# Zero products of 28 columns instead of 506 in the score accumulator of a conv and attention kernel

## The chip, the core and the metric

One core of a Trainium2 chip runs the whole program in one launch. The metric is device time in microseconds (us), from the start to the end of an execution. A run's time is one such execution, and the time before is the median of three.

Four engines work side by side, each through its own queue in order: TensorE (PE; weight loads are shown apart as PEld), VectorE (DVE), ScalarE (ACT) and GpSimd (POOL). SyncE (SP) issues most DMAs.

## The reference

Sixteen images of 128 channels and 28x28 pixels pass through four layers: an L1-distance convolution, two 3x3 convolutions with quantised weights and activations, then on 784 tokens an image an additive attention with a mixture of experts, and a linear attention with a spectral filter. The change concerns the scores of the additive attention:

```python
def _L2_attn_ref(B, W, v):
    Wi = jnp.einsum('bnd,ed->bne', B, W)
    scores = jnp.einsum('d,bijd->bij', v, jnp.tanh(Wi[:, None, :, :] + Wi[:, :, None, :]))
    attn = jax.nn.softmax(scores, axis=-1)
    C = jnp.einsum('bij,bjd->bid', attn, B)
    return C
```

A score is symmetric in i and j, so that half of them are enough.

## The kernel before

**Stages.** The images go in pairs. For each pair the distance convolution makes taps on DVE (lines 1139 and 1141) and ACT (line 1137), and PE sums them (line 1126). Beside the distances of a later pair, the remaining layers of earlier images are woven in: the quantised convolutions, the scores, the attention, the experts, the linear attention and the spectral filter (lines 1019 and 1022). In the trace the scores begin at 1156 us. From about 10390 us on no distances are left, and the code calls that stage "alone".

**Buffers.** Taps and, in the stage alone, blocks of tanh values share a ring of 10 buffers (RING). Rows of tanh values have 14 (ROWS). The score accumulator `sp` is one bank of the on-chip accumulation memory (PSUM, which PE writes and DVE and ACT read): 128 partitions x 512 columns, taken anew from a pool of one buffer for every block.

**Scores of one image.** `wi` holds the 784 projected tokens and, after them, the first 504 again. `scores(b)` walks through NT = 7 blocks of TB = 112 tokens. A block is four groups of Q = 28 tokens, and group j has the 32 partitions from 32j on. For m = 0 to 27 the four tokens Qj + m of a block each get a row: tanh of `wi` over a window of WIN = 394 columns that begins at the token itself. Beside the distances ACT makes the rows one by one (line 727), with the token as bias. In the stage alone DVE adds (line 720) and ACT takes the tanh of four rows at once (line 722). `products_of` multiplies the row by v on PE (line 710). The slice of `vz` that is loaded as weights has v in column m and zeros elsewhere, so that partition m of the group receives the row and the other 31 have zeros added. The product lands on columns Qj + m to Qj + m + 393.

**The first row of a block.** As each row lands one column further right than the one before, the accumulator has to be defined over all columns first. At m = 0, four products with zero weights (line 706) are written with `start=True` over all 506 columns, one to each group; the row products then only add.

**The end of a block.** After m = 27 DVE multiplies the 504 columns `sp[:, :SPAN]` by a mask `near` into `sc` (line 738, and line 740 where the window runs over the end of the image). The next block's zero products overwrite the same bank, so they wait for this.

**Order.** The lanes of the planner (`Lane`, `rows`, `ahead`, `behind`) lay down a traced order of all work: taps of the next step, PE sums of this one, products that are due, then other lanes. `in_traced_order` (line 1179) pins that order on PE alone. On DVE, ACT and SP the build chooses the order, from its own estimate of when instructions are ready.

Of the kernel before, what the change touches and what calls it, by code (L numbers as in the profile page):

```python
# [8 lines left out]
F32 = mybir.dt.float32  # L9
# [8 lines left out]
P = 128  # L18
# [46 lines left out]
TB, NT, Q = 112, 7, 28  # L65
# [3 lines left out]
WIN = T // 2 + 2  # L69
SPAN = T // 2 + TB  # L70
# [69 lines left out]
def cols(ap, lo, n):  # L140

    return ap[:, lo // Q * 32 : (lo + n) // Q * 32].rearrange("p (n c) -> p n c", c=32)[:, :, :Q]


def in_rows(ap):

    return ap.rearrange("p (n c) -> p n c", c=Q)
# [23 lines left out]
def kernel(ctx: ExitStack, tc: tile.TileContext, a: dict, out: bass.AP):  # L171
    nc = tc.nc
# [8 lines left out]
    pss = ctx.enter_context(tc.tile_pool(name="pss", bufs=1, space=PSUM))  # L181
# [21 lines left out]
    def slot(n, name):  # L203
        return ring.tile([P, 4 * WIN], F32, tag="d", name=name)[:, :n]
# [215 lines left out]
    vz = const.tile([P, 64], F32, name="vz")  # L420
# [271 lines left out]

    products = []

    def scores(b):


        while b not in state:
            yield
        wi = state[b][3]  # L700

        def products_of(sp, ib, m, rows):
            if m == 0:

                for j in range(4):
                    nc.tensor.matmul(sp[32 * j : 32 * j + 32, : SPAN + 2], vz[:, :32],  # L706
                                     wi[:, ib * TB : ib * TB + SPAN + 2], start=True, stop=False, skip_group_check=True)
            for j in range(4):
                lo = Q * j + m
                nc.tensor.matmul(sp[32 * j : 32 * j + 32, lo : lo + WIN], vz[:, 32 - m : 64 - m], rows[j],  # L710
                                 start=False, stop=m == Q - 1, skip_group_check=True)

        for ib in range(NT):
            sp = pss.tile([P, 512], F32, tag="sp", name=f"sp{b}_{ib}")
            for m in range(Q):
                i = ib * TB + m
                if stage["alone"]:
                    th = slot(4 * WIN, f"th{b}_{ib}_{m}").rearrange("p (a b) -> p a b", b=WIN)
                    for j in range(4):
                        nc.vector.tensor_scalar(th[:, j, :], wi[:, i + Q * j : i + Q * j + WIN],  # L720
                                                wi[:, i + Q * j : i + Q * j + 1], None, ALU.add)
                    nc.scalar.activation(th, th, AF.Tanh)  # L722
                    rows = [th[:, j, :] for j in range(4)]
                else:
                    rows = [rows_pool.tile([P, WIN], F32, tag="row", name=f"row{b}_{i + Q * j}") for j in range(4)]
                    for j in range(4):
                        nc.scalar.activation(rows[j], wi[:, i + Q * j : i + Q * j + WIN], AF.Tanh,  # L727
                                             bias=wi[:, i + Q * j : i + Q * j + 1])
                products.append(lambda sp=sp, ib=ib, m=m, rows=rows: products_of(sp, ib, m, rows))
                yield  # L730
            while products:
                products.pop(0)()
            while ib == 0 and b and b - 1 not in attended:
                yield
            lo = ib * TB
            n = min(SPAN, T - lo)
            dst = sc[:, ib, :]
            nc.vector.tensor_tensor(cols(dst, lo, n), in_rows(sp[:, :n]), in_rows(near[:, :n]), ALU.mult)
            if n < SPAN:
                nc.vector.tensor_tensor(cols(dst, 0, SPAN - n), in_rows(sp[:, n:SPAN]), in_rows(near[:, n:]), ALU.mult)  # L740
        scored.add(b)
# [308 lines left out]
    for b in range(B):  # L1050
        chain.add(attend(b), experts(b), linear_attention(b), normed(b)) if b + 1 == B else chain.add(
            *([head(1)] if b == 0 else []), attend(b), experts(b), linear_attention(b), normed(b),
            *([head(b + 2)] if b + 2 < B else []))
        conv_out.add(spectral(b))
    units = [scores(b) for b in range(B)]
    due = {"units": 0.0}

# [157 lines left out]
```

## Time and profile before

| what | us |
|---|---|
| median of three runs | 12013.93 |
| lowest and highest run | 12013.17, 12015.77 |
| the profiled execution's own time | 12013.72 |
| its span, first to last instruction | 12012.0 |
| DVE busy | 10731.9 |
| ACT busy | 10263.3 |

The profile is of one execution, and the span leaves out 1.72 us around the instructions. Busy time of PE is a union of pipelined matmuls whose ends are modelled, so it is more than the time in which PE streams columns. Of an instruction group the profile gives its line, engine, operands, shape and count; every float32 product stands there as two matmuls, each with a weight load. Thus 448 zero products (16 images x 7 blocks x 4 groups) are 896 matmuls of line 706, eight to a block, and there are 112 blocks.

### The profile page before, as it was taken

What the parts mean: (1) busy time and instruction counts of PE and PEld (TensorE: products, weight loads), DVE (VectorE), ACT (ScalarE), POOL (GpSimd) and SP (SyncE); (2) the same over time, 40 slices, a digit from 0 to 9 for tenths busy, and PEclk for the clock granted to TensorE, in tenths of its full rate; (3) what the DMA queues carried; (4) which work ended last, traced back from release to release, by engine and by line L of the source; (5) the groups of instructions that cost most, each with busy time, mean ns of one, the idle gap of its engine ahead of it and who ended that gap; (6) DMA issues with size and microseconds to landing.
All of it is one profiled execution on the core that took longest, in us unless ns stands there. A gap on an engine that the chain in (4) does not pass through costs nothing. (4 is left out here: it accounts for less than half of the span.)

```text
span 12012.0 us, 240466 instructions
## 1 busy us (share of the span) xinstructions
PE 11409.5 (95%) x99948; PEld 5214.0 (43%) x99948; DVE 10731.9 (89%) x15051; ACT 10263.3 (85%) x14568; POOL 186.2 (2%) x144
## 2 busy tenths in 40 slices
PE   8989999999999999999999999999999999999999
PEld 3333333444444444444444444444444444454446
DVE  9898789899999999899999999999999889988882
ACT  8884998979979899797998979889898898988882
POOL 0000000000000000000000000000000000000000
PEclk9999999999999999999999999999999999999999
DMA  0110000010110101001010110101110111011113
GB/s 24 58 32 5 1 1 6 17 34 27 33 32 18 35 28 32 24 28 33 26 38 17 31 33 25 31 26 31 34 31 19 29 31 34 27 54 51 54 54 97
DMA packets 376034, 372.49 MB, mean 31 GB/s; under 512 B 40296, under 2 KB 362144, under 8 KB 374944
## 3 DMA queue, kind: packets, MB, share of 16 engines
q1 hardware_dynamic: 374512, 355.35, 10.4%
q8 instruction: 787, 12.89, 0.4%
q14 instruction: 303, 2.48, 0.1%
q10 hardware_dynamic: 432, 1.77, 0.0%
HBM read 340.19 MB, written 16.78 MB: 30 GB/s over the span
## 5 line engine op out<-in xcount | busy, mean ns | idle before, releaser
L727 ACT ACTIVATE row<-wi 128x394 f32<-128x394 f32 x9904 | 5297.0, 625 | 254.1 <-PE sp L710 251.8
L1126 PE MATMUL acc<-d,sel_m 128*32 128x392 f32 x38656 | 5217.3, 502 | 144.2 <-DVE d L1141 133.3
L1139 DVE TENSOR_SCALAR d<-pad,w 128x1568 f32<-128x1568 f32 x4832 | 4783.5, 1031 | 456.9 <-PE acc L1126 454.3
L1126 PE MATMUL acc<-d,sel_a 128*32 128x392 f32 x18176 | 4502.8, 500 | 71.1 <-ACT d L1137 68.8
L1137 ACT ACTIVATE d<-pad,w 128x1568 f32<-128x1568 f32 x2272 | 3581.7, 1609 | 597.7 <-PE acc L1126 581.0
L1141 DVE SCALAR_TENSOR_TENSOR d<-pad,w,d 128x1568 f32<-128x1568 f32 x2112 | 3863.1, 1846 | 8.7
L1126 PEld LDWEIGHTS acc<-d,sel_m 128*32 128x32 f32 x38656 | 1714.0, 111 | 2121.2 <-issue 1653.9
L710 PE MATMUL sp<-row,vz 128*32 128x394 f32 x19808 | 2086.9, 495 | 1.1 <-ACT row L727 1.1
L1126 PEld LDWEIGHTS acc<-d,sel_a 128*32 128x32 f32 x18176 | 1349.4, 110 | 1111.1 <-issue 857.7
L1019 PE MATMUL u<-band,up 128*128 128x392 f32 (+3 forms) x8192 | 1752.9, 355 | 16.4 <-ACT us L1029 14.0
L1019 PEld LDWEIGHTS u<-band,up 128*128 128x128 f32 x8192 | 1330.0, 190 | 964.6 <-issue 281.2
L710 PEld LDWEIGHTS sp<-row,vz 128*32 128x32 f32 x19808 | 728.1, 110 | 1052.9 <-issue 791.1
L722 ACT ACTIVATE th<-th 128x1576 f32<-128x1576 f32 x660 | 969.8, 1521 | 118.4 <-DVE th L720 109.7
L720 DVE TENSOR_SCALAR th<-wi 128x394 f32<-128x394 f32 x2640 | 923.3, 420 | 12.0 <-PE sp L710 9.2
L1022 PE MATMUL out<-us,mat 128*128 128x392 f32 (+1 forms) x2048 | 923.6, 534 | 0.0
L1029 ACT COPY us<-u 128x392 f32<-128x392 f32 x1024 | 491.4, 480 | 480.6 <-PE u L1019 478.5
L710 PE MATMUL sp<-th,vz 128*32 128x394 f32 x5280 | 514.1, 503 | 47.7 <-ACT th L722 47.5
L884 DVE SCALAR_TENSOR_TENSOR t<-ex,gate,t 128x128 f32<-128x128 f32 x896 | 310.7, 347 | 83.9 <-PE ex L880 75.7
L1022 PEld LDWEIGHTS out<-us,mat 128*128 128x128 f32 x2048 | 311.7, 192 | 21.3 <-issue 8.3
L710 PEld LDWEIGHTS sp<-th,vz 128*32 128x32 f32 x5280 | 136.8, 109 | 340.7 <-issue 168.0
L880 PE MATMUL ex<-ew,xt 128*128 128x512 f32 x448 | 236.0, 609 | 37.1 <-DVE t L884 33.2
L795 PE MATMUL av<-vx,sc 128*128 128x129 f32 x1568 | 202.4, 282 | 37.3 <-DVE sc L784 18.7
(257 smaller groups left out, 4415.9 us busy)
## 6 DMA issues: line engine op xcount, KB each, us to landing
band<-band SPq DMA_DIRECT2D x1024, 196.0 KB, 2.4
mat<-mat SPq DMA_DIRECT2D x1024, 64.0 KB, 2.0
L_conv_w<-q_L_conv_w SPq DMA_DIRECT2D x16, 576.0 KB
ew<-in_L_ffn_expert_w_dram SPq DMA_DIRECT2D x16, 512.0 KB
eb<-eb_rows SPq DMA_DIRECT2D x16, 448.0 KB, 4.2
x<-in_x_dram SPq DMA_DIRECT2D x8, 784.0 KB
band<-band_out SPq DMA_DIRECT2D x32, 196.0 KB, 1.9
xr<-in_x_dram SPq DMA_DIRECT2D x8, 784.0 KB, 4.1
```

The lines of the kernel that those rows point to most:

```text
L710: nc.tensor.matmul(sp[32 * j : 32 * j + 32, lo : lo + WIN], vz[:, 32 - m : 64 - m], rows[j], start=False, stop=m == Q - 1, skip_group_chec ...
L720: nc.vector.tensor_scalar(th[:, j, :], wi[:, i + Q * j : i + Q * j + WIN], wi[:, i + Q * j : i + Q * j + 1], None, ALU.add)
L722: nc.scalar.activation(th, th, AF.Tanh)
L727: nc.scalar.activation(rows[j], wi[:, i + Q * j : i + Q * j + WIN], AF.Tanh, bias=wi[:, i + Q * j : i + Q * j + 1])
L884: nc.vector.scalar_tensor_tensor(t[:, i, :], q[:, e * P : (e + 1) * P], gate[:, g : g + 1], t[:, i, :], ALU.mult, ALU.add)
L1019: nc.tensor.matmul(q[:, P * i : TH], up[:, to ^ odd, i, :], t[:, :w], start=i == 0, stop=i == 3)
L1022: nc.tensor.matmul(acc[:, lag:TH], m0, u[:, : TH - lag], start=False, stop=n is None and not copied)
L1029: nc.scalar.copy(u[:, :TH], q[:, :TH])
L1126: nc.tensor.matmul(accs[c][32 * j : 32 * j + 32, :NCK], sel[kind][:, 31 - m : 63 - m], d[:, 14 * c : 14 * c + 14, :], start=False, stop=n ...
L1137: nc.scalar.activation(d, window(pad, k, 0, 2 * HW), AF.Abs, bias=w0[:, k, f : f + 1], scale=-1.0)
L1139: nc.vector.tensor_scalar(d, window(pad, k, 0, 2 * HW), w0[:, k, f : f + 1], None, ALU.max)
L1141: nc.vector.scalar_tensor_tensor(d, window(pad, k, 0, 2 * HW), w0[:, k, f : f + 1], d, ALU.max, ALU.add)
```

## The change

The zero products cover 28 columns a group instead of 506: the columns Qj + 394 to Qj + 421, which the first row does not reach and later rows of the group do. The first row's products are now written with `start=True`. The accumulator is one fixed tile for the whole kernel, cleared once by DVE, and columns that no product of a group reaches keep that zero. The number of products is the same, and so are the rows, the weights and the mask multiplication.

```diff
+    sp = pss.tile([P, 512], F32, name="sp")
+    nc.vector.memset(sp, 0.0)
+
     def scores(b):
...
-        def products_of(sp, ib, m, rows):
-            if m == 0:
-
-                for j in range(4):
-                    nc.tensor.matmul(sp[32 * j : 32 * j + 32, : SPAN + 2], vz[:, :32],
-                                     wi[:, ib * TB : ib * TB + SPAN + 2], start=True, stop=False, skip_group_check=True)
+        def products_of(m, rows):
+            for j in range(4):
+                if m == 0:
+
+
+                    hi = Q * j + WIN
+                    nc.tensor.matmul(sp[32 * j : 32 * j + 32, hi : hi + Q], vz[:, :32], wi[:, :Q],
+                                     start=True, stop=False, skip_group_check=True)
             for j in range(4):
                 lo = Q * j + m
                 nc.tensor.matmul(sp[32 * j : 32 * j + 32, lo : lo + WIN], vz[:, 32 - m : 64 - m], rows[j],
-                                 start=False, stop=m == Q - 1, skip_group_check=True)
+                                 start=m == 0, stop=m == Q - 1, skip_group_check=True)
 
         for ib in range(NT):
-            sp = pss.tile([P, 512], F32, tag="sp", name=f"sp{b}_{ib}")
             for m in range(Q):
...
-                products.append(lambda sp=sp, ib=ib, m=m, rows=rows: products_of(sp, ib, m, rows))
+                products.append(lambda m=m, rows=rows: products_of(m, rows))
```

## The prediction

> **What bounds the kernel now.** I read the page's busy times first, then its chain of waits, then the costliest groups, and then went to the blocks' first rows.
>
> ```profile
> PE 11409.5 (95%) x99948; PEld 5214.0 (43%) x99948; DVE 10731.9 (89%) x15051; ACT 10263.3 (85%) x14568; POOL 186.2 (2%) x144
> PE 30%; DVE 11%; ACT 5%; issue 1%; POOL 0%; DMA 0%; POOLq 0%; ACTq 0%; DVEq 0%
> L727 ACT ACTIVATE row<-wi 128x394 f32<-128x394 f32 x9904 | 5297.0, 625 | 254.1 <-PE sp L710 251.8
> L1126 PE MATMUL acc<-d,sel_m 128*32 128x392 f32 x38656 | 5217.3, 502 | 144.2 <-DVE d L1141 133.3
> L1139 DVE TENSOR_SCALAR d<-pad,w 128x1568 f32<-128x1568 f32 x4832 | 4783.5, 1031 | 456.9 <-PE acc L1126 454.3
> L1137 ACT ACTIVATE d<-pad,w 128x1568 f32<-128x1568 f32 x2272 | 3581.7, 1609 | 597.7 <-PE acc L1126 581.0
> ```
>
> All three engines are close to full, PE most. DVE stood still for 454 us and ACT for 581 until PE freed a tap buffer; PE stood still for 133 until DVE had made a tap. So PE leads, but not alone. The chain's shares add up to 47% because the trace could be followed back only to about 6400 us; of those 47 points PE has 30, DVE 11 and ACT 5. Less PE work is therefore worth more than half its length, and not all of it.
>
> Next, the matmuls by shape, of the whole span:
>
> ```profile
> L710 PE MATMUL sp<-row,vz 128*32 128x394 f32 x19808 | 2086.9, 495 | 1.1 <-ACT row L727 1.1
> L706 PE MATMUL sp<-wi,vz 128*32 128x506 f32 x896 | 124.8, 590 | 6.3 <-DVE sc L740 5.9 <-DVE sc L738 0.3
> ```
>
> The zero products almost never wait (6.3 us in all): DVE has usually emptied the bank in time. Then the chain of waits around one block's start shows what four zero products cost PE:
>
> ```profile
> 9323.25 2.77 PE acc L1126 x32
> 9326.02 0.85 PE sp L706 x8
> 9326.87 1.32 PE sp L710 x16
> 9328.19 1.65 PE u L1019 x8
> ```
>
> Columns: start, length, line, matmuls. The eight matmuls take 0.85 us from start to start, as PE runs the four groups together: their modelled durations (590 ns each) overlap. I asked for the chain at each of the 38 block starts from 6400 to 10390 us, and 21 had this picture; at the others DVE or ACT carried the chain. In the stage alone:
>
> ```profile
> by line: PE sp L710 27.9%; PE u L1019 24.4%; PE out L1022 11.3%; DVE th L720 10.8%; ACT th L722 5.1%; PE ex L880 2.9%; PE av L795 2.5%; issue 1.6%; PE sp L706 1.3%; PE conv_ps L395 1.1%; DVE mx L771 0.7%; PE qk L909 0.7%; PE tc_n L646 0.6%;
> ```
>
> 1.3% of these 1300 us (10390 to 11690) is 16.9 us, which is 20 of the stage's 23 blocks at 0.85 us.
>
> **What the Trainium skill says.** (1) "TensorE: Matmul & The Clock Gate", section "Wait — 56ns, not 53.3ns?": two matmuls never start less than about 25 ns apart, however short. Inside a group of four this trace has starts within 0.02 us of each other for four (1150.80 to 1150.82 us in the timeline)[...], so I use 25 ns for a bound alone. (2) Same page, "The mechanism": weight loads pass running matmuls only where the row group differs. The trace says otherwise for column groups: four loads for the rows stand in 0.13 us of PEld beside running sums. (3) "PSUM — Partial Sum Buffer", "The four PSUM rules": a starting matmul clears the written-marks of its whole bank in its quadrant, but not the data. So the first row's start clears the marks that the zero products just set, and the second row overwrites a zero where it would have added to one. By that page the sums come out the same; no run here shows it yet. (4) Same page, "PSUM bank collisions raise a hardware error": PE must not write a bank and quadrant that DVE reads. So the 28-column products need the same wait on lines 738 and 740 as the 506-column ones.
>
> **The change part by part.**
>
> *Zero products.* Of line 706 and line 710 the mean matmuls are 590 and 495 ns, or 587 and 494 by the medians of the two lines' own views: 93 ns for 112 columns, 0.83 ns a column. 506 columns stream for 420 ns, twice for the two matmuls of a product: 0.84 us, as the chain's 0.85 says. 28 columns stream for 23 ns, 0.05 us in all. No row of the trace has so short a product on 32 columns of weights. From below the cost is 0.05 us, if weight loads and starts hide. From above it is two rounds of weight loads, 2 x 0.13 = 0.26 us; eight starts at the page's 25 ns would be 0.20, an estimate. I take 0.15. The quad gets shorter by 0.70 us (0.59 to 0.80), and 112 of them by 78 us of PE (66 to 90).
>
> *What of this reaches the end.* Beside the distances there are 89 blocks (712 matmuls by the windows' counts), of which 21/38 = 55% lie on the chain: 89 x 0.55 x 0.70 = 34 us. For the first 51 blocks I use the same share, since PE is about as busy there (943 to 972 us of each 1000 between 2000 and 9000 us). In the stage alone 20 x 0.70 = 14 us. Together 48 us, if no parallel path takes over. One does, in part. A saving passes from PE to DVE only as far as DVE had been waiting: the waits of line 1139 are 454.3 us over 375 times, 1.2 us each. Where PE's next wait is for DVE (133.3 us over 117 times, 1.1 each) or for a row of ACT, the saving is simply waited away. Both happen within a few microseconds of a block's start. I let 0.6 of the 48 through, a choice between 0.2 (nearly all lost at the next wait) and 1: 29 us.
>
> *Start flag on the first row, narrower reading of `wi`, one fixed bank.* Nothing: the row products have the same columns, PE's in-order queue separates them from the zeros, and the one buffer of the pool was the same bank already. The wait for DVE moves along with the zero products. Queued behind it on PE are the four rows of m = 0 and then sums; today it costs 6.3 us in the whole span, and could be up to 0.70 us longer where PE now arrives earlier, which is in the 0.6.
>
> *The clearing.* One DVE instruction on 512 columns near the start; its nearest row, the mask multiplication of 504 columns, takes 0.68 us. It is done long before 1156 us. At most 0.7 us, with DVE's taps queued behind it; I put it at nothing.
>
> *Order on DVE and ACT.* PE's order is pinned, the others' are not, and the build works them out from estimates that include PE's length. The trace shows that it departs from the written order:
>
> ```profile
> 1486.61 0.62 DVE L738 TENSOR_TENSOR sc<-sp,near 128x448 f32<-128x448 f32 x1 [7.34 <-PE sp L710]
> 1487.16 1.03 DVE L1139 TENSOR_SCALAR d<-pad,w 128x1568 f32<-128x1568 f32 x1
> 1488.10 0.21 DVE L740 TENSOR_TENSOR sc<-sp,near 128x56 f32<-128x56 f32 x1
> ```
>
> A tap of 1.03 us stands between lines 738 and 740, which follow each other in the code. A shorter quad can move such a tap or a row at any of the 112 blocks, for better or worse; I take zero, with 30 us either way for the range.
>
> Sum: the profiled execution's 12013.72 (span 12012.0 and 1.72 around it), less 29, is 11984.7. The median shown is 0.21 above the profiled execution, so 11985.
>
> **The rivals.**
>
> *A, part of the chain's worth (forecast): 11985.* For it: PE's 30 of 47 points, 21 of 38 block starts. Against: so many short waits both ways. Its own range, 0.2 to 0.9 of the 48 us with the quad's bounds: 11966 to 12004.
>
> *B, all of it or more: 48 to 60 us, 11958.* PE would have to lead nearly everywhere. DVE and ACT waited for PE far longer than PE for them, which speaks for it; DVE at 92 to 94% busy beside the distances speaks against.
>
> *C, waited away: 12007.* DVE is the true limit beside the distances, and the quad only brings PE sooner to its next wait. Then only about half of the stage alone's 14 us is left. For it: 17 of 38 block starts were not on PE's chain. Against: DVE's 454 us of waiting.
>
> *D, slower: 12041.* The build's new order puts a tap of line 1139 (1.03 us) ahead of what PE needs next, at DVE's queue around the block's start, in half of the blocks: 112 / 2 x 1.03 = 58 us lost against 29 gained, net 29 slower. It decides from a mean loss of 29 / 112 = 0.26 us a block on. For it: the order of 1487 us above. Against: nothing that prefers bad places to good ones.
>
> **How the numbers follow.** A 0.45, B 0.17, C 0.16, D 0.22. About 0.2%, 24 us, is what a measurement can tell from no change here. A is beyond that in 0.72 of its cases (0.32) and B in all: faster 0.49. C with the rest of A and the small end of D: same 0.27. The larger part of D and its tail: slower 0.24. The range runs from B's far end with 30 us of order luck, 11930, to D with some 15 more, 12055; one in twenty is left out below, some three in twenty above.
>
> **What would show it.** Right: line 706 as 28-column matmuls whose eight take 0.1 to 0.25 us from start to start; PE's busy time some 70 us lower; line 1139's wait for PE lower, and PE's waits for DVE and ACT higher by 30 to 50 us; equal counts on every line. Wrong: a quad above 0.4 us (the floor mis-sized), line 706 waiting far more than 6.3 us for lines 738 and 740, or PE's busy time down with the span unchanged (C). For D, DVE and ACT queues in another order and new waits of line 1126 or line 710.

## The result, and the profile after

The changed kernel takes 11972.85 us (median of 6 runs, 11971.38 to 11975.57) against 12014.41 us before (6 runs, 12013.17 to 12018.26). The ratio is 0.9965, with a 95% interval of 0.9953 to 0.9978: faster by 42 us, where 29 were forecast. The profiled execution took 11972.2 us with a span of 11970.3. Lines behind the change stand four to five numbers further down: 706 is now 711, 710 is 715, 722 is 726, 1126 is 1130, 1137 is 1141 and 1139 is 1143.

The page after, busy time and the two groups that wait for tap buffers:

```profile
PE 11347.5 (95%) x99948; PEld 5198.5 (43%) x99948; DVE 10727.9 (90%) x15052; ACT 10260.9 (86%) x14568; POOL 186.8 (2%) x144
L1143 DVE TENSOR_SCALAR d<-pad,w 128x1568 f32<-128x1568 f32 x4832 | 4780.7, 1030 | 438.2 <-PE acc L1130 429.0
L1141 ACT ACTIVATE d<-pad,w 128x1568 f32<-128x1568 f32 x2272 | 3578.9, 1608 | 570.0 <-PE acc L1130 555.2
```

PE does as many matmuls as before, and DVE one instruction more, the clearing. DVE and ACT work as long as before. What got shorter is the wait of these two groups for PE, by 25 and 26 us (454.3 and 581.0 before). Matmuls by shape show the edit itself:

```profile
L711 PE MATMUL sp<-wi,vz 128*32 128x28 f32 x896 | 31.3, 194 | 6.1 <-DVE sc L744 5.8 <-DVE sc L742 0.3
```

The matmuls' wait for the mask multiplication is as it was (6.1 us, before 6.3), now on a 28-column matmul. The chain of waits around one block's start (columns: start, length, line, matmuls):

```profile
9294.38 2.77 PE acc L1130 x32
9297.15 0.06 PE sp L711 x8
9297.20 1.33 PE sp L715 x16
```

The neighbours have kept their lengths (2.77, and 1.33 for 1.32), and the eight zero matmuls take 0.06 us from start to start, where they took 0.85. That is 0.79 us a block, 88 us over the 112 blocks if each is like this one. So 42 of 88 us reached the end.

Where? The tanh over four rows marks the beginning of the stage alone, in which no distances are left. Its line in the views of that line, before and after (the numbers after the colon are the shortest, median and longest in ns, then come first and last start in us):

```profile
core 0 of [0], span 12012.0 us
L722 ACT ACTIVATE th<-th x660: 1499/1519/1580, 10385.7 to 11676.0; 128x1576 f32<-128x1576 f32 x165
```

```profile
core 0 of [0], span 11970.3 us
L726 ACT ACTIVATE th<-th x660: 1495/1519/1580, 10346.4 to 11635.4; 128x1576 f32<-128x1576 f32 x165
```

The stage begins 39.3 us earlier, and from there to the end it lasts 1626.3 us before and 1623.9 after. Nearly the whole gain arises beside the distances. The stage in which 20 of 23 blocks' zero products lay on the chain gives 2.4 us. That was not forecast, and the experiments start from it.

One thing besides the edit itself had changed. PE's order is pinned, but on ACT 790 of some 14,600 instructions, and on DVE some 2,100 of 15,052, stand elsewhere in the queue than before: on ACT nearly all by one to five places, on DVE three in four of them. The two causes, shorter products and another order, can be taken apart, since an order can be prescribed.

### The profile page after: what moved, and what is told of

Same layout as the page of the kernel before. It is cut to its first block, busy times and chain, and to the rows that moved or that the text cites. A ratio compares the mean times of both kernels' runs of the same rounds, so it can differ in the third digit from the quotient of the medians.

```text
span 11970.3 us, 240357 instructions
## 1 busy us (share of the span) xinstructions
PE 11347.5 (95%) x99948; PEld 5198.5 (43%) x99948; DVE 10727.9 (90%) x15052; ACT 10260.9 (86%) x14568; POOL 186.8 (2%) x144
## 5 line engine op out<-in xcount | busy, mean ns | idle before, releaser
L715 PE MATMUL sp<-th,vz 128*32 128x394 f32 x5280 | 517.8, 504 | 58.8 <-ACT th L726 58.4
```

## The experiments

The theory was that the shorter zero products bring the gain by themselves, by a fixed part of each microsecond saved; its rivals, that the new order on DVE and ACT takes a good part of the gain away, or brings it.

### One cause at a time

Both orders were written into kernels as lists, for DVE, ACT and SP, in the way the code pins PE:

```diff
     in_traced_order(tc, (mybir.EngineType.PE,))
+    in_given_order(tc)
```

```python
for engine, text in GIVEN.items():
...
    for k, by in enumerate(moved):
        i = mine[k + by]
        if last is not None:
            tc.add_manual_dep(
                i, last,
                mybir.DependencyInfo(mybir.DependencyClass.NoSync, mybir.DependencyReason.DATA), reason="order",
            )
        last = i.name
```

The changed kernel in the order of the kernel before:

> The changed kernel, with DVE, ACT and SP held to the order in which the build of the kernel before put them. Theory (the shorter zero products do it, the new order nothing): as the changed kernel, 11973, between 11966 and 11980, with the stage alone (about 1298 us) again no shorter. Rival 1 (the new order gave part of the gain away, above all in the stage alone): about 11960 or less, the stage alone some 12 us shorter. Rival 2 (the new order brought part of the gain): 11985 or more.

Measured: 11983.06 us against 12015.69, ratio 0.9973 (0.9962 to 0.9984): 32.6 us faster. That is neither what the theory said nor what the first rival did; it lies 2 us from what the second said, that the new order brought part of the gain.

The kernel before in the order of the changed one:

> The kernel before with its 506-column zero products, with DVE, ACT and SP held to the order of the changed kernel's build. Theory (order is worth nothing): 12014, between 12007 and 12021. Rival 1 (the new order costs): 12026 or more. Rival 2 (it gains by itself): 12002 or less.

Measured: 12014.20 us against 12015.69, ratio 0.9999 (0.9990 to 1.0007), as the theory said. On the long products the new order is worth nothing in sum, within an interval of some 10 us either way.

```profile
core 0 of [0], span 12012.3 us
L722 ACT ACTIVATE th<-th x660: 1494/1519/1568, 10381.7 to 11677.1; 128x1576 f32<-128x1576 f32 x165
```

The stage alone begins 4.0 us earlier than before and lasts 1630.6 us, 4.3 longer. These are single executions, so whether the sum hides a small gain and a small loss stays open.

The fixed bank and its clearing alone:

```diff
+    sp = pss.tile([P, 512], F32, name="sp")
+    nc.vector.memset(sp, 0.0)
...
-            sp = pss.tile([P, 512], F32, tag="sp", name=f"sp{b}_{ib}")
```

> The kernel before with one fixed bank, cleared once, and the 506-column zero products as they were. Theory: the bank is worth nothing, 12014, between 12009 and 12019. Rival (the fixed bank spares waits on PE, whose line of zero products has 51 semaphore instructions of 51 ns before the change and 3 after): 2.6 us or more faster, down to about 12005.

Measured: 12016.06 us against 12015.69, ratio 1.0000 (0.9992 to 1.0009). The semaphore instructions of the zero products' line, 51 ns each, do fall from 51 to 3 with the bank alone, but no gain is measured: the theory held.

The changed kernel beside the others again:

> The changed kernel itself, beside the others on one chip. All theories: 11973, between 11969 and 11980. What it is for: if it stands below the run with short products in the old order (11983) by 5 us or more again, the new order is worth that much; if the two are level, it is not.

Measured: 11972.91 us against 12015.22, ratio 0.9966 (0.9953 to 0.9978). It is 10 us below the run with the short products in the old order (11983.06), as the changed kernel in the result was (11972.85). The old order was measured on another chip, and the intervals of the two ratios overlap, but no execution of the one kernel does with those of the other: at most 11977.79 us here and at least 11979.08 there, while the kernel before differs by 0.5 us between the two. So 42 us are some 33 from the edit and some 9 from the new order, which on the long products brought 1.5 us, within the noise. The run in the old order shows where the 9 come from:

```profile
core 0 of [0], span 11977.4 us
L726 ACT ACTIVATE th<-th x660: 1497/1519/1603, 10360.1 to 11641.4; 128x1576 f32<-128x1576 f32 x165
```

In the old order the stage alone begins 25.6 us earlier than before and lasts 1617.3 us, 9.0 less than before. The new order therefore helps by 13.7 us beside the distances and costs 6.6 us in the stage alone (single executions; this one is 4 us below its kernel's median). PE's waits for the tanh in that stage agree. The first two lines are of the kernel before, 10392 to 11690 us; the next two of the changed kernel, 10353 to 11650 us; the last two of the run in the old order, 10366 to 11656 us. Columns: total us, times, longest.

```profile
PEld sp L710 <- ACT th L722: 137.2, 171, 3.0
PE sp L710 <- ACT th L722: 47.5, 76, 2.3
```

```profile
PEld sp L715 <- ACT th L726: 158.7, 196, 3.0
PE sp L715 <- ACT th L726: 58.4, 94, 2.5
```

```profile
PEld sp L715 <- ACT th L726: 144.0, 176, 3.0
PE sp L715 <- ACT th L726: 52.7, 81, 2.5
```

With the short products PE waits longer for ACT in this stage than before, and in the new order longer than in the old.

### Both orders, each where it is good

If the reading by stage holds, the new order up to the stage alone and the old order from there on must be faster than either. The lists of DVE and ACT were joined at the first tanh of four rows.

> The changed kernel with the orders of DVE and ACT of its own build up to the stage alone, and those of the build before from there on. Theory (beside the distances the new order helps by 14 us, in the stage alone it costs 6): 11966, between 11961 and 11971. Rival (the two orders' effects aren't a matter of the stage, single profiles mislead): as the changed kernel, 11973, or above.

Measured: 11965.75 us against 12015.22, ratio 0.9959 (0.9946 to 0.9971).

```profile
core 0 of [0], span 11964.0 us
L726 ACT ACTIVATE th<-th x660: 1498/1519/1599, 10346.8 to 11629.7; 128x1576 f32<-128x1576 f32 x165
```

It begins the stage alone where the changed kernel does and lasts there, at 1617.2 us, what the run in the old order does. A second session:

> The mixed order once more, with the 28-column zero products. Theory (its 11966 was the order's doing): 11966 again, between 11961 and 11970, 7 us below the changed kernel. Rival (the first session was a lucky one, and orders this alike differ by chance between sessions): 11971 or above.

Measured: 11968.34 us against 12015.28, ratio 0.9961 (0.9947 to 0.9974). That is what the theory said, and again no execution overlaps with the changed kernel's (at most 11969.83 against at least 11971.38). With 4.5 to 7 us below the changed kernel this is the fastest version tried. It was put together from two orders after the fact; whether another edit would ask for another one was not tried.

The views of the tanh's line in the changed kernel's second profile and in this last run:

```profile
core 0 of [0], span 11972.1 us
L726 ACT ACTIVATE th<-th x660: 1494/1519/1585, 10348.3 to 11637.4; 128x1576 f32<-128x1576 f32 x165
```

```profile
core 0 of [0], span 11968.1 us
L726 ACT ACTIVATE th<-th x660: 1497/1520/1570, 10350.8 to 11633.7; 128x1576 f32<-128x1576 f32 x165
```

All profiles with 28 columns in every block, side by side:

| order of DVE and ACT | stage alone begins, us | lasts, us |
|---|---|---|
| new (the changed kernel, twice) | 10346.4, 10348.3 | 1623.9, 1623.8 |
| old | 10360.1 | 1617.3 |
| new, then old (twice) | 10346.8, 10350.8 | 1617.2, 1617.3 |

The length of the stage alone follows the order to 0.1 us in five profiles. Its beginning follows the order too, with some 4 us of spread. The lists by themselves cost nothing visible: with a prescribed new order the stage alone begins where it does in the changed kernel, whose order on DVE and ACT is the build's own.

### What a microsecond of PE is worth

In the old order, with 267 of the 506 columns:

```diff
-                    hi = Q * j + WIN
-                    nc.tensor.matmul(sp[32 * j : 32 * j + 32, hi : hi + Q], vz[:, :32], wi[:, :Q],
+                    nc.tensor.matmul(sp[32 * j : 32 * j + 32, :267], vz[:, :32], wi[:, :267],
```

> The changed kernel in the old order of DVE, ACT and SP, with zero products of 267 columns (the first 267 of the bank), which is 0.40 us a block or 45 us of PE less than with 506, half of the full step of 88. Theory (of each us of PE a fixed part, 0.37 as in the run with short products in the old order, reaches the end): 16 us faster than the kernel before, 11999. Rival 1 (a small saving passes nearly whole where PE leads, 0.62 of it, and only a larger one is cut off by the waits): 28 us faster, 11988. Rival 2 (small savings are waited away): under 8 us faster, 12007 or more.

Measured: 11997.66 us against 12015.22, ratio 0.9986 (0.9979 to 0.9992): 17.6 us of 45, 0.39 of each (0.21 to 0.56 by the interval). The theory holds in this order, and both rivals, 28 us and under 8, lie outside.

The other way, in the kernel before:

```diff
-                for j in range(4):
+                for j in [*range(4), *range(4)]:
                     nc.tensor.matmul(sp[32 * j : 32 * j + 32, : SPAN + 2], vz[:, :32],
```

> The kernel before in its own order with every zero product issued twice, 0.84 us a block or 94 us of PE more. Theory (a fixed part, 0.37): 35 us slower than before, 12050. Rival (adding work makes PE lead more often, so that added time counts at the chain's share of 0.62 or more): 58 us slower or more, 12073.

Measured: 12074.80 us against 12015.22, ratio 1.0050 (1.0037 to 1.0064): 59.6 us of 94, 0.63 of each. The theory is wrong here, and the rival's number comes out: what is added counts at the chain's share (54.5 of 88 us, 0.62, worked out below), what is taken away in this order at some 0.6 of it. The pages show where the difference lies, though not why. First PE with doubled zeros, then with the short products in the old order:

```profile
PE 11495.2 (95%) x100844; PEld 5241.0 (43%) x100844; DVE 10735.1 (89%) x15051; ACT 10268.9 (85%) x14568; POOL 185.1 (2%) x144
PE 11358.0 (95%) x99948; PEld 5194.0 (43%) x99948; DVE 10728.0 (90%) x15052; ACT 10260.1 (86%) x14568; POOL 187.0 (2%) x144
```

Of its span (12071.9 us and 11977.4 us) PE is not busy for 577 us with the doubled zeros and for 619 with the short ones; before it was 602. So work that was added filled 26 us in which PE had stood idle. Of the work that was removed, 17 us became idle time, and some 37 more neither left the span nor became idle time: presumably they lie in pauses between matmuls that the page, whose ends are modelled, counts as busy. That fits a PE that arrives early and finds the others not ready, but no run shows it.

Nor is the asymmetry shown for other orders. The old order was worked out for the long products. In the mixed order the short products gain 47 to 50 us of 88, 0.53 to 0.56 of each, not far from the 0.63 of the doubled ones. No run doubled the zero products in an order of their own.

In the stage alone only:

```diff
-                    hi = Q * j + WIN
-                    nc.tensor.matmul(sp[32 * j : 32 * j + 32, hi : hi + Q], vz[:, :32], wi[:, :Q],
+                    hi, n = (Q * j + WIN, Q) if stage["alone"] else (0, SPAN + 2)
+                    nc.tensor.matmul(sp[32 * j : 32 * j + 32, hi : hi + n], vz[:, :32], wi[:, :n],
```

> The kernel before in its own order with 28-column zero products in the 23 blocks of the stage alone and 506 columns in the 89 before; the bank is fixed. Theory (half of these 23 x 0.79 = 18 us is waited away for ACT's tanh): 9 us faster than before, 12006. Rival 1 (the chain's share there, 20 of 23, holds): 16 us faster, 11999. Rival 2 (all is waited away): 12015.

Measured: 12008.14 us against 12015.74, ratio 0.9994 (0.9985 to 1.0002): 7.6 us. The middle value fits the theory, but the interval leaves room for both rivals.

```profile
core 0 of [0], span 12004.1 us
L726 ACT ACTIVATE th<-th x660: 1496/1519/1595, 10387.6 to 11669.5; 128x1576 f32<-128x1576 f32 x165
```

The profile is clearer: the stage alone lasts 1616.5 us, 9.8 less than before, next to the 9.0 of the first run. So about half of the 18 us passes in this stage. The run shows one thing more. Its 89 blocks beside the distances have the start flag on the first row, read `wi` from its first column and use the fixed bank; only the 506 columns are as before. The stage alone begins no earlier than before (10387.6 against 10385.7 us), so these three bring nothing there, and what the short products gain beside the distances in the same order comes from their length.

### No zero products at all

By the Trainium skill, "PSUM — Partial Sum Buffer", section "The four PSUM rules" (the second), the first row's start clears the marks of its whole bank in the quadrant (the 32 partitions of its group), and later rows then overwrite what it did not reach. So the zero products can be left out, and in the three runs that follow the scores come out right without them:

```diff
-            for j in range(4):
-                if m == 0:
-
-
-                    hi = Q * j + WIN
-                    nc.tensor.matmul(sp[32 * j : 32 * j + 32, hi : hi + Q], vz[:, :32], wi[:, :Q],
-                                     start=True, stop=False, skip_group_check=True)
```

> The changed kernel without any zero product: the first row still starts its group, and the later rows write the columns that it does not reach. Theory: of the changed kernel's 0.06 us a block, 6.7 us of PE, about half is on the path to the end: 3 us faster than the changed kernel, 11970. Rival (weight loads and the wait for DVE before the zero products cost more than their 0.06 us): 10 us faster or more, 11963 or less.

Measured: 11980.06 us against 12015.69, ratio 0.9971 (0.9961 to 0.9981), 7 us slower than the changed kernel where 3 faster were expected. Its build had moved some 500 DVE instructions against the changed kernel's, so the orders were pinned, first the changed kernel's, then the mixed one:

> The changed kernel without any zero product, with DVE, ACT and SP held to the order of the changed kernel's build. Theory (the run without zero products was slower than the changed kernel because its build put DVE and ACT in another order): 0.06 us a block gone, 0.37 of it on the path, so 2 to 3 us faster than the changed kernel, 11970. Rival (the zero products themselves help PE, by loading weights or by waiting for DVE early): as the run without them, 11980.

> The same in the mixed order (its own build's before the stage alone, the build before's in it). Theory: 2 to 3 us faster than the mixed order with zero products, 11963. Rival (the zero products themselves help): 11972 or above.

Measured: 11973.65 us (ratio to before 0.9967, 0.9955 to 0.9979) and 11975.70 us (0.9967, 0.9954 to 0.9979). In the first case some 6 of the 7 us are gone, which points to the order, as the theory said (the two kernels' executions overlap, though); the 2 to 3 us of gain that were expected are too few to be told from nothing here. In the second case the kernel is 7 to 10 us slower than with zero products, as the rival said. By the profiles the loss arises in the stage alone: it begins at 10346.8 us in both, and lasts 1622.0 us in place of 1617.2. One difference stands in the view of the row products' line, first without zero products in the mixed order, then with them:

```profile
L708 PEldq EVENT_SEMAPHORE  x64: 51/51/51, 1236.0 to 11593.5; - x64
```

```profile
L715 PEldq EVENT_SEMAPHORE  x6: 51/51/51, 10692.8 to 11094.1; - x6
```

Without zero products the first row has to wait for DVE and for ACT, and 58 more of its waits stand as an instruction of their own at 51 ns, 3.0 us in all, against the 112 x 0.06 = 6.7 us that were saved. But with the fixed bank alone 48 such instructions went and no time went with them, so this does not explain the loss. Why the kernel in the mixed order gets slower without zero products stays open.

## Why the prediction was right

**What bounds the kernel.** Right: PE leads, with DVE and ACT close behind. DVE's and ACT's busy times stayed, and the waits of their taps for PE fell.

**Length of the short quad.** A term that was mis-sized. I took 0.15 us between 0.05 and 0.26, and named 0.1 to 0.25 as the sign; it is 0.06, next to the pure streaming of 0.05. The two rounds of weight loads (110 ns each) hide beside the matmuls, and the saving is 0.79 us a block and 88 us in all, not 0.70 and 78.

**Share on the chain and what passes.** With 0.79 in place of 0.70, the sum reads 89 x 0.55 x 0.79 = 38.7 beside the distances and 20 x 0.79 = 15.8 in the stage alone, 54.5 together, and 0.6 of it is 32.7 us. In the old order 32.6 us were measured, and by the marks of the stages 25.6 and 9.0, that is 0.66 and 0.57 (of an execution 4 us below the median). That it agrees so closely is in part luck: the 0.6 was a choice between 0.2 and 1, and the share for the first 51 blocks was carried over from the later ones. The other orders show that 0.6 is no constant. In the mixed order the stage alone begins 35 to 39 us earlier than before, so that beside the distances nearly the chain's whole worth passes, and in the stage alone 9.1 of 15.8. The doubled products show that it doesn't hold for adding, in the old order.

**Start flag, narrower reading, fixed bank, clearing.** Put at nothing, and nothing was measured for the bank with its clearing (12016.06 against 12015.69). The start flag and the reading of `wi` were not tried alone, but together with the bank they gained nothing beside the distances in the run with short products in the stage alone only.

**Order.** Put at nothing, with 30 us either way; it brings 9 us in sum, some 14 gained and 7 lost by the profiles. So the forecast of 29 and the measured 42 us differ by 4 us for the length of the quad and 9 us for the order, and the forecast's division by stage (20 beside, 8 alone) did not come: it was 39 and 2. An order that costs time exists in the stage alone, with 7 us, but not by rival D's mechanism: no tap of line 1139 stands in that stage, and PE waits there for ACT's tanh. I had not seen that the order's effect has a stage and a sign of its own.

**The rivals.** B, all of the chain's worth, is 55 us with the measured quad. The old and the new order stay well below; the mixed one, with 47 to 50 us, comes near. C does not hold: the gain beside the distances is the larger one.

**What was to be seen.** PE's busy time fell by 62 us (some 70 said). Of PE's waits only 19 us were added (matmuls of line 1126 from 215.3 to 222.7 us, of line 710 with `th` from 47.7 to 58.8), less than the 30 to 50 said. Of the 88 us, 42 reached the end and some 20 became idle time of PE (span less busy time: 602.5 us before, 622.8 after); the remaining 26 presumably lie in pauses between matmuls that the page counts as busy.

## What to carry to other kernels

Where several engines run close together, price an edit on the leading one by the share of its sites on the chain of waits, and leave a range for the near-parallel paths: here 0.6 to 0.9 of the chain's worth passed when work was removed, by the order of the other queues, and all of it when work was added. Where only one queue is pinned, an edit of a length can reshuffle the others, as it did here: hold their order to tell the two apart before explaining a gain of this size, and look at each stage, since a sum can hide a gain and a loss. An instruction that does nothing useful may still carry a wait for its successor, so look at the waits before leaving it out.

## What the runs showed of the hardware

Eight matmuls of 28 columns, two to each of the four groups of 32 weight columns, need 0.06 us from the first start to the next row's, under 8 ns each, though each is shown with 192 ns and has its own weight load of 110 ns. The 25 ns between starts that the Trainium skill gives ("TensorE: Matmul & The Clock Gate", "Wait — 56ns, not 53.3ns?") is no floor across column groups here. It may still be one within a group: in most blocks of the changed kernel's trace the second matmul of a group starts 28 or 29 ns after its first.

In this kernel, work added to PE cost 0.63 us for each us. Work removed at the same places in the same order saved 0.37 to 0.39, and in the mixed order 0.53 to 0.56.
